# A threshold guess taken as a logarithm, its guards moved to VectorE, and a packed list's flags made by one comparison

## The chip, the cores and the metric

The kernel runs on one core of one Trainium2 chip. The metric is the device time of one execution in microseconds, lower is better. Engines are named as in the profile: PE (TensorE, with PEld for its weight loads), DVE (VectorE), ACT (ScalarE), POOL (GpSimd) and SP (SyncE, which here only issues transfers).

## The reference

A graph layer over 3327 nodes with 256 features each, run twice (two steps). In each step every node attends to all nodes, but only to its nucleus: the most probable nodes whose probabilities first reach 0.9 together. A sparse adjacency matrix diffuses the features beside it.

```python
h = jnp.maximum(_layernorm(x), 0.0)
Xf = Xa = h;  R = adj + eye;  R = R / R.sum(-1, keepdims=True)
for n in range(2):
    q = Xa @ W1.T @ W2.T;  k = Xa @ W3.T
    probs = softmax(q @ k.T)
    sp = sorted(probs, descending);  cs = cumsum(sp)
    keep = cs - sp < 0.9                       # the nucleus of each row
    A = probs * keep;  A = A / max(A.sum(-1, keepdims=True), 1e-12)
    Xf = R @ Xf
    Xa = A @ Xa
    Z = Z + Xf @ U1[n].T + Xa @ U2[n].T
return x + layernorm(h + Z) * ln_g + ln_b
```

All arithmetic is float32.

## The kernel before

**Tiles.** The nodes stand in 26 tiles of 128 rows, padded to 3328. A tile's attention row block is a 128 x 3328 array `e` of exponentials, made by matmuls (L600) and exponentials on ScalarE (L604 to L610).

**The nucleus without a sort.** For each tile the kernel guesses a threshold per row. `guessed` (L616) works out a first estimate from the row's sum of exponentials Z and from moments of the scores. Then ScalarE scans the whole row block against that estimate (`through`, L631, seen in the profile as L633): with Relu and with Sign, each with a sum. In the first step (`measured_once`, L635) these two sums give the guess col(16) by a short chain of one-column instructions; in the second step (`measured_twice`, L668) a third scan is made. The columns col(k) are the columns of one small tile `g` for each tile.

VectorE then clears everything at or over the guess and sums the rest (L729, in `settle`), takes the eight largest of each of 20 segments (L734), merges them (L738 to L753), and so finds the exact threshold; L763 clears `e` under it. If a guess was unfit for any row, a flag starts a slow layer that searches (`search_graph_layer`); the executions shown here do not enter it.

**The sum.** `Sums` transposes the cleared row block in seven parts on TensorE (L809), ScalarE copies each out (`eT`, L811), and TensorE multiplies it with the features (L823).

**The adjacency.** `listed` (L836) reads the adjacency matrix of each tile and lists per row the columns' blocks in which it has entries, up to 16; four are used directly. What is over these four is packed into one further list of 128 for the tile: L865 counts a row's entries, `packed` (L870) sums the counts over the rows before by a matmul and makes a 128 x 128 array of flags `oh` (which row a place of the packed list belongs to) by two comparisons on VectorE (L879, L880), `gathered` (L882) turns this into an index by a matmul. Indirect transfers that POOL issues then fetch the rows: `adjacent` (L896, seen as L900) and `fetched` (L917, seen as L921), five each for a tile. `diffuse` (L926) multiplies them.

**The order of the work** is written out by hand. In each iteration i of the loop at L1160 there are seven slots; a string for each slot (`PLAN` L1136, with others for the first and last iterations, L1141) names generators, and each letter runs one of them to its next `yield`:

- m: `measured` for tile i+1; d and c: `settle` for tile i and for the one before
- w and q: `weights` for tile i+3; e: `first_end` (L937), which ends tile i-2 (its copy `sv` L945 on ScalarE, the addition L946 on POOL)
- s: `spread`, the diffusion; a: `listed`; p: `packed` for tile i+1; h: `gathered` for tile i; g: one indirect transfer; o: a tile's own rows

After the letters of a slot a part of `Sums` is turned and one is summed. Each engine executes its instructions in the order in which this text issues them (L1232 makes that order binding for TensorE, ScalarE, VectorE and POOL, and in the first step for SP's queue). An indirect transfer issued by g also waits for the last ScalarE instruction that the text issued before it (L1206 to L1209).

For a tile of the first step `measured_once` has five segments. In the slots of `PLAN[0]`, counted from 0, they stand so: the estimate and its POOL columns in slot 0, the Relu scan in slot 1, the Sign scan in slot 3, the ScalarE chain L653 to L659 in slot 4, the five VectorE instructions L662 to L666 in slot 6. `settle` starts with L729 in slot 0 of the next iteration, and its L763 stands in slot 5.

Of the kernel before, what the change touches and what calls it, by code (L numbers as in the profile page):

```python
# [9 lines left out]
F32 = mybir.dt.float32  # L10
# [3 lines left out]
AF = mybir.ActivationFunctionType  # L14
ALU = mybir.AluOpType
# [3 lines left out]
P = 128  # L19
# [4 lines left out]
NP = NT * P  # L24
# [6 lines left out]

SCALE = 1.9
BITS = 27
FIRST = 2.0 ** -7
assert 0.1 * SCALE / N > 2.0 ** -15


# [1 line left out]
def search_graph_layer(  # L39
# [13 lines left out]
    nc = tc.nc  # L53
# [94 lines left out]
    def nucleus(es, z):  # L148
# [10 lines left out]
        nc.vector.memset(cand, FIRST)  # L159
# [153 lines left out]
BIG = 1.0e30  # L313
# [3 lines left out]
ROUNDS = (5, 6)  # L317
PG = (0.72168716, 3.51308980, -3.48705157)
PK = (3.57528079, -2.54929187, 0.86603878)
OFFSET = (18.0, 14.0)  # L320
TOPK = 8 * max(ROUNDS)
LNY = 0.25 * math.log(0.72)

# [6 lines left out]
FIRST = 8 * P  # L330
# [15 lines left out]
def guess_graph_layer(ctx, tc, x, adj, w1t, w2t, w3t, u1t, u2t, ln_g, ln_b, out, flag):  # L346
# [66 lines left out]
    one = const.tile([P, 8], F32, tag="one", name="one")  # L413
    for k, c in enumerate((1.0, -1.0, 5.0e-4, SQG[1], SQK[1], math.log(10.0), LNY, 1.0e-12)):
# [213 lines left out]
    def con(k):  # L628
        return one[:, k : k + 1]
# [5 lines left out]
    def measured_once(r):  # L635
        e, ms = r["e"], r["ms"]


        col = guessed(r, small.tile([P, 17], F32, tag="g", name="g"))
        S.activation(col(4), col(2), AF.Square, bias=con(4))  # L640
        S.activation(col(11), col(4), AF.Identity, scale=ms(5), bias=ms(6))
        S.activation(col(1), col(0), AF.Exp, scale=-1.0, bias=con(5))
        G.tensor_scalar(col(7), col(9), 0.5, None, ALU.mult)
        G.tensor_scalar(col(8), col(9), 0.5 * NP, None, ALU.mult)
        G.tensor_scalar(col(5), col(1), OFFSET[0], None, ALU.mult)
        G.tensor_scalar(col(10), col(9), col(5), 1.0, ALU.mult, ALU.add)
# [189 lines left out]
    def listed():  # L836
        pieces = [(t, j0, min(size, NT - j0)) for t in range(NT) for size in (HALF if t < HALVES else AD,)
                  for j0 in range(0, NT, size)]

        def asked(t, j0, n):  # L840
            at = (roomy[(2 * t + j0 // HALF) % 4] if t < HALVES else
                  adjp.tile([P, AD, P], F32, tag="at", name="at", bufs=2))
            nc.sync.dma_start(at[:, :n], adj[t, :, j0 : j0 + n, :])
            return at

        ahead = asked(*pieces[0])
        for k, (t, j0, n) in enumerate(pieces):
# [12 lines left out]
            V.max(ls[:, :8], fm)  # L860
            V.match_replace(fm, ls[:, :8], fm, 0.0)
            V.max(ls[:, 8:LIST], fm)
            G.tensor_scalar(index[:, t, :DIRECT], ls[:, :DIRECT], -1.0, float(NONE), ALU.mult, ALU.add)
            of = small.tile([P, LIST], F32, tag="of", name="of", bufs=2)
            V.tensor_scalar(of[:, DIRECT:], ls[:, DIRECT:LIST], 0.0, None, ALU.is_gt, ALU.add,  # L865
                            accum_out=over[:, t : t + 1])
            done.append(t)
            yield

    def packed(t):  # L870

# [4 lines left out]
        S.copy(ls[:, LIST:], pb[:, 0, :1])  # L876
        yield
        ohs[t] = oh = small.tile([P, P], F32, tag="oh", name="oh", bufs=2)
        V.tensor_scalar(oh, place, ov, ls[:, LIST:], ALU.subtract, ALU.is_lt)  # L879
        V.scalar_tensor_tensor(oh, place, ls[:, LIST:], oh, ALU.is_ge, ALU.mult)  # L880

    def gathered(t):  # L882
        oh = ohs.pop(t)
# [7 lines left out]
        yield  # L891
        of = small.tile([P, LIST], F32, tag="of", name="of", bufs=2)
        V.scalar_tensor_tensor(of[:, :n], place[:, :n], nth, lo, ALU.is_equal, ALU.mult, accum_out=nth)
        G.tensor_scalar(index[:, t, DIRECT:], nth, -1.0, float(NONE), ALU.mult, ALU.add)

    def adjacent(t):  # L896
# [83 lines left out]
        V.tensor_copy(flag, pf[:1, 0, :1])  # L980

    own_of = {}
    live, ohs, acs, xgs, done, early = {}, {}, {}, {}, [], {}
    none = iter(())

    def run(work, n=99):
# [139 lines left out]
    def refetch(t):  # L1126
# [14 lines left out]
    BEGIN = {-1: ("mba", "mmbba", "mwwbbaa", "bmwwb", "", "", ""),  # L1141
             0: ("mdbba", "mcdbba", "medbwwbap", "mdabb", "gmpdbwwba", "hgdabgbq", "hgq"),
             1: ("ggmdsssbba", "gmcdgsssbba", "gedbawwbp", "msdbga", "gmpdeag", "hgdawwqg", "hgemgqo"),
             2: ("gmdsssa", "gmcdsssga", "gedawwpg", "gmsdga", "gmspdea", "ohgdawwqg", "gehmgq")}
# [136 lines left out]
```

## Time and profile before

| what | value |
|---|---|
| median of 3 runs | 1354.68 us (1349.92 to 1356.13) |
| profiled execution, its own time | 1350.64 us |
| its span | 1348.9 us |
| busy: PE, DVE, ACT, POOL | 1268.1, 1186.8, 1081.0, 997.2 us |
| granted TensorE clock, mean | 0.982 |

The span is the time from the first to the last instruction of the profiled execution. Busy time is an engine's own; an engine may be busy and still wait for nothing, or idle and hold up nobody. The row of a group or of an instruction names line, engine, operation, what is written from what, and times. In the timeline the first number is the start in microseconds from the start of the span, the second the length; an idle time in front of an instruction is added in brackets with what ended it.

The first step fills the span from about 75 to 735 us; before it the features are normed and multiplied, from about 800 us the second step runs.

### The profile page before, as it was taken

The page shows a single profiled execution, that of the slowest core. Times are in us where ns is not written, and L with a number is a line of the kernel's source. Part 1 is how long each engine was busy: PE and PEld are TensorE (multiplying, and loading weights), DVE is VectorE, ACT ScalarE, POOL GpSimd, SP SyncE. Part 2 cuts the span into 40 slices and gives each one's busy share as a digit, 9 for nine tenths or more (in the row PEclk, how much of TensorE's full clock was granted, in tenths as well). Part 3 has the DMA queues.
Part 4 walks back from the last instruction along what each step waited for, and adds up shares of the span by engine and source line. Part 5 has one row for each costly group of instructions (what it writes and reads, how often), then busy time and mean ns, then how long its engine had stood idle before and what let it go on. Part 6 is the DMA issues. An engine that isn't in the chain of part 4 may idle for free.

```text
span 1348.9 us, 22270 instructions
## 1 busy us (share of the span) xinstructions
PE 1268.1 (94%) x6495; PEld 976.0 (72%) x6495; DVE 1186.8 (88%) x3637; ACT 1081.0 (80%) x2368; POOL 997.2 (74%) x1399
## 2 busy tenths in 40 slices
PE   5989899999999999999999579999999999999985
PEld 4635687877778777787877457777777777777774
DVE  6877899999999999999990689899998999999993
ACT  5475788798888879888863789899998999999841
POOL 5114788888878878887873578888888888888832
PEclk9999999999999999999999779999999999999998
DMA  8644545455454544445332212221212222122200
GB/s 277 221 157 141 160 136 144 134 144 147 133 153 133 140 138 142 144 135 152 106 104 86 75 55 60 78 89 54 91 59 85 62 82 90 52 91 64 81 21 24
DMA packets 92645, 149.79 MB, mean 111 GB/s; under 512 B 15425, under 2 KB 59072, under 8 KB 92512
## 3 DMA queue, kind: packets, MB, share of 16 engines
q1 hardware_dynamic: 75056, 105.37, 24.6%
q0 software_dynamic: 16640, 42.69, 12.1%
q8 instruction: 54, 0.88, 0.3%
q14 instruction: 79, 0.65, 0.2%
q10 hardware_dynamic: 816, 0.20, 0.1%
HBM read 120.93 MB, written 27.28 MB: 110 GB/s over the span
## 4 chain that ended last, share of the span: by engine, by line
PE 51%; DVE 20%; ACT 12%; POOL 11%; issue 3%; DMA 2%; SPq 0%; POOLq 0%; DVEq 0%; ACTq 0%
PE pa L823 22%; ACT ja L633 7%; PE pl L600 7%; PE pt L809 6%; PE pr L929 5%; POOL xg L921 5%; DVE w L729 4%; PE pz L942 3%; DVE cand L734 3%; DVE e L763 3%; PE pz L1011 2%; POOL g L676 2%; DVE bb L741 1%; DVE cand L743 1%; ACT e L604 1%
## 5 line engine op out<-in xcount | busy, mean ns | idle before, releaser
L823 PE MATMUL pa<-xw,eT 128*128 128x256 f32 x1352 | 323.6, 384 | 3.6 <-DVE s L953 3.6
L633 ACT ACTIVATE ja<-e,g 128x3328 uint8<-128x3328 f32 x106 | 325.7, 3072 | 0.1
L823 PE MATMUL pa<-x,eT 128*128 128x256 f32 x1352 | 323.1, 380 | 0.0
L823 PEld LDWEIGHTS pa<-xw,eT 128*128 128x128 f32 x1352 | 250.7, 190 | 52.5 <-issue 14.4
L823 PEld LDWEIGHTS pa<-x,eT 128*128 128x128 f32 x1352 | 243.7, 191 | 25.8
L734 DVE MAX8 cand<-w 128x8 f32<-128x168 f32 (+1 forms) x1040 | 253.7, 319 | 0.0
L811 ACT COPY eT<-pt 128x512 f32<-128x512 f32 (+1 forms) x364 | 199.5, 555 | 48.8 <-PE pt L809 47.7
L921 POOL DMA_INDIRECT xg<-bx,index x130 | 188.7, 1451 | 54.7 <-issue 24.4
L900 POOL DMA_INDIRECT ac<-in_adj,index x130 | 162.9, 1253 | 63.8 <-issue 28.2
L809 PE MATMUL pt<-ident,e 128*128 128x128 f32 x1144 | 176.6, 277 | 17.3 <-DVE e L760 9.4
L809 PEld LDWEIGHTS pt<-ident,e 128*128 128x128 f32 x1144 | 139.8, 144 | 60.5 <-issue 36.0
L921 POOL DMA_INDIRECT xg<-vx,index x130 | 152.5, 1173 | 34.3 <-issue 30.3
L729 DVE SCALAR_TENSOR_TENSOR w<-e,g 128x3328 f32<-128x3328 f32 x44 | 162.7, 3698 | 3.1 <-ACT g L714 3.0
L929 PE MATMUL pr<-xg,ac 128*128 128x257 f32 (+1 forms) x520 | 141.0, 395 | 8.4 <-DVE s L1119 6.8
L763 DVE SCALAR_TENSOR_TENSOR e<-e,rec 128x3328 f32<-128x3328 f32 x40 | 148.3, 3707 | 0.6
L604 ACT ACTIVATE e<-pl 128x832 f32<-128x832 f32 x132 | 112.9, 859 | 27.3 <-PE pl L600 21.9
L929 PEld LDWEIGHTS pr<-xg,ac 128*128 128x128 f32 x520 | 93.9, 194 | 34.0 <-issue 14.1
L600 PE MATMUL pl<-both,qT 64*128 64x416 f32 x416 | 93.0, 546 | 9.3 <-ACT e L604 7.0
L741 DVE MAX8 bb<-cand 128x8 f32<-128x160 f32 x286 | 92.7, 324 | 6.4
L853 DVE TENSOR_REDUCE fm<-at 128x4 f32<-128x512 f32 (+1 forms) x133 | 84.7, 637 | 13.3 <-DMA at<-in_adj 13.3
L600 PE MATMUL pl<-after,qT 64*128 64x416 f32 x416 | 95.4, 552 | 0.5 <-ACT e L604 0.5
L633 ACT ACTIVATE ja<-x,g 128x3328 uint8<-128x3328 f32 x24 | 73.7, 3070 | 0.0
(260 smaller groups left out, 2129.8 us busy)
## 6 DMA issues: line engine op xcount, KB each, us to landing
at<-in_adj SPq DMA_DIRECT2D x114, 256.0 KB
cx<-ac SPq DMA_DIRECT2D x26, 384.0 KB
ac<-cx SPq DMA_DIRECT2D x26, 384.0 KB
wide<-in_adj SPq DMA_DIRECT2D x8, 832.0 KB
e<-in_adj SPq DMA_DIRECT2D x6, 832.0 KB
own<-bx SPq DMA_DIRECT2D x26, 128.5 KB
x<-in_x SPq DMA_DIRECT2D x13, 256.0 KB
xr<-in_x SPq DMA_DIRECT2D x26, 128.0 KB
```

The source lines that it names most:

```text
L600: PE.matmul(pl[:, a, :wd], qT[p, :], keys_of(step, a).rearrange("p a b -> p (a b)")[:, c : c + wd], start=True, stop=True)
L604: S.activation(e.rearrange("p (a n) -> p a n", a=2)[:, :, c : c + wd], pl[:, :, :wd], AF.Exp, accum_out=za[:, n : n + 1])
L633: S.activation(ja, e, f, bias=guess, scale=sign, accum_out=total)
L729: V.scalar_tensor_tensor(w, e, col(16), e, ALU.is_lt, ALU.mult, accum_out=d2)
L734: V.max(cand[:, 8 * s : 8 * s + 8], w[:, s * SEG : min(NP, (s + 1) * SEG)])
L763: V.scalar_tensor_tensor(e, e, at(1), e, ALU.is_ge, ALU.mult, accum_out=ra)
L809: PE.transpose(pt[:, j, :], e[:, (j0 + j) * P : (j0 + j + 1) * P], ident)
L811: S.copy(eT[:, :w, :], pt[:, :w, :])
L823: PE.matmul(self.pa, eT[:, c - 4 * k, :], self.xa[:, j, :], start=c == 0, stop=c == NT - 1)
L900: G.indirect_dma_start(out=ac[:, k, :], out_offset=None, in_=rows, in_offset=bass.IndirectOffsetOnAxis(ap=index[:, t, k : k + 1], axis=0), ...
L921: G.indirect_dma_start(out=xg[:, k, :w], out_offset=None, in_=rows, in_offset=bass.IndirectOffsetOnAxis(ap=index[:, t, k : k + 1], axis=0))
L929: PE.matmul(pr[:, :w], ac[:, k, :], own if k == KT - 1 else xg[:, k, :w], start=k == 0, stop=k == KT - 1)
```

## The change

In the first step the guess is formed as a logarithm. Before, ScalarE took a power by Ln and Exp of a difference, and VectorE then limited it, multiplied it with the estimate and added guards (a huge number where the row is not to be cut). Now the logarithm of col(10) is taken by ScalarE behind the Relu scan (L654), the guards are made by three VectorE instructions (L663 to L665) as amounts to be subtracted from an exponent of at most 80, and ScalarE forms Relu and Exp from them (L666, L667). Four columns are added on POOL (L643, L648 to L650). The last segment moves from slot 6 to slot 5 and so stands ahead of `settle`'s clearing pass (L763 before, L764 after).

For the packed list the count of L865 on VectorE becomes a Sign with a sum on ScalarE (`counted`, L874), followed by two POOL instructions that make two limits of it (L876, L877). `gathered` for tile t runs it for tile t+2, in slot 6. In `packed` ScalarE adds one more instruction (L887) and a square over 128 x 128 places (L889), and VectorE makes the flags by one comparison (L891) in place of two.

One constant changes (18 to 19), and a name in the layer that is not entered. The line numbers of the changed kernel are higher by up to 13 from there on.

```diff
@@ measured_once
         S.activation(col(1), col(0), AF.Exp, scale=-1.0, bias=con(5))
+        G.tensor_scalar(col(11), col(11), -1.0, None, ALU.mult)
         G.tensor_scalar(col(7), col(9), 0.5, None, ALU.mult)
         G.tensor_scalar(col(8), col(9), 0.5 * NP, None, ALU.mult)
         G.tensor_scalar(col(5), col(1), OFFSET[0], None, ALU.mult)
         G.tensor_scalar(col(10), col(9), col(5), 1.0, ALU.mult, ALU.add)
+        G.tensor_scalar(col(12), col(3), ms(3), ms(8), ALU.mult, ALU.add)
+        G.tensor_scalar(col(12), col(12), -1.0, 80.0, ALU.mult, ALU.add)
+        G.tensor_scalar(col(13), r["Z"], 0.035, None, ALU.mult)
         yield
         oa = small.tile([P, 3], F32, tag="oa", name="oa")
         through(e, AF.Relu, col(9), -1.0, oa[:, 0:1])
+        S.activation(col(10), col(10), AF.Ln)
         yield
         through(e, AF.Sign, col(9), -1.0, oa[:, 1:2])
         yield
         S.activation(col(3), oa[:, 0:1], AF.Identity, scale=-1.0, bias=col(8))
         S.activation(col(4), oa[:, 1:2], AF.Relu, scale=col(7), bias=col(3))
         S.activation(col(6), col(4), AF.Ln, scale=col(1), bias=con(2))
-        S.activation(col(3), col(4), AF.Square, scale=col(1), bias=con(1))
-        S.activation(col(3), col(3), AF.Ln, scale=0.5, bias=col(10))
-        S.activation(col(3), col(3), AF.Identity, scale=-1.0, bias=col(6))
-        S.activation(col(3), col(3), AF.Exp, scale=col(11))
-        yield
-
-        V.tensor_scalar(col(5), oa[:, 1:2], NP - 31.0, BIG, ALU.is_gt, ALU.mult)
-        V.tensor_scalar(col(6), col(4), col(1), 0.35, ALU.mult, ALU.is_lt)
-        V.scalar_tensor_tensor(col(5), col(6), BIG, col(5), ALU.mult, ALU.add)
-        V.tensor_scalar(col(3), col(3), 1.0e20, col(9), ALU.min, ALU.mult)
-        V.tensor_tensor(col(16), col(3), col(5), ALU.add)
+        S.activation(col(10), col(10), AF.Identity, scale=-1.0, bias=col(6))
+        yield
+        V.tensor_scalar(col(5), oa[:, 1:2], NP - 31.0, 60.0, ALU.is_gt, ALU.mult)
+        V.tensor_scalar(col(14), col(4), col(13), 60.0, ALU.is_lt, ALU.mult)
+        V.scalar_tensor_tensor(col(12), col(12), col(5), col(14), ALU.subtract, ALU.subtract)
+        S.activation(col(10), col(10), AF.Relu, scale=col(11), bias=col(12))
+        S.activation(col(16), col(10), AF.Exp, scale=-1.0, bias=con(8))
@@ listed
-            of = small.tile([P, LIST], F32, tag="of", name="of", bufs=2)
-            V.tensor_scalar(of[:, DIRECT:], ls[:, DIRECT:LIST], 0.0, None, ALU.is_gt, ALU.add,
-                            accum_out=over[:, t : t + 1])
@@ new, and packed
+    def counted(t):
+
+        if t not in done or t in nhs:
+            return
+        of = small.tile([P, LIST], F32, tag="of", name="of", bufs=2)
+        ov = over[:, t : t + 1]
+        S.activation(of[:, DIRECT:], lists[:, t, DIRECT:LIST], AF.Sign, accum_out=ov)
+        nhs[t] = nh = small.tile([P, 3], F32, tag="nh", name="nh", bufs=4)
+        G.tensor_scalar(nh[:, 0:1], ov, -0.5, 0.5, ALU.mult, ALU.add)
+        G.tensor_scalar(nh[:, 1:2], ov, ov, 0.25, ALU.mult, ALU.mult)
     def packed(t):
-        assert t in done
+        counted(t)
+        nh = nhs[t]
...
         S.copy(ls[:, LIST:], pb[:, 0, :1])
-        yield
+        S.activation(nh[:, 2:3], pb[:, 0, :1], AF.Identity, scale=-1.0, bias=nh[:, 0:1])
         ohs[t] = oh = small.tile([P, P], F32, tag="oh", name="oh", bufs=2)
-        V.tensor_scalar(oh, place, ov, ls[:, LIST:], ALU.subtract, ALU.is_lt)
-        V.scalar_tensor_tensor(oh, place, ls[:, LIST:], oh, ALU.is_ge, ALU.mult)
+        S.activation(oh, place, AF.Square, bias=nh[:, 2:3])
+        yield
+        V.tensor_scalar(oh, oh, nh[:, 1:2], None, ALU.is_lt)
@@ gathered, behind its V.scalar_tensor_tensor
+        if valid(t + 2):
+            counted(t + 2)
@@ the order of the first step (the same in BEGIN 0 to 2)
-    PLAN = (("gmdsssa", "gmcdsssa", "edawwpg", "gmsdga", "gmspdea", "ohgdawwqg", "gehmgq"),
+    PLAN = (("gmdsssa", "gmcdsssa", "edawwpg", "gmsdga", "gmspdea", "ohgmdawwqg", "gehmgq"),
```

More of the change, by code (lines that the diff above doesn't have):

```diff
@@ L33 @@
 BITS = 27
-FIRST = 2.0 ** -7
+LOWEST = 2.0 ** -7
 assert 0.1 * SCALE / N > 2.0 ** -15
@@ L158, in nucleus @@
         nc.vector.tensor_scalar(thr, z, TOP_P, None, ALU.mult)
-        nc.vector.memset(cand, FIRST)
+        nc.vector.memset(cand, LOWEST)
         for k in range(BITS - 1, -1, -1):
@@ L319 @@
 PK = (3.57528079, -2.54929187, 0.86603878)
-OFFSET = (18.0, 14.0)
+OFFSET = (19.0, 14.0)
 TOPK = 8 * max(ROUNDS)
@@ L412, in guess_graph_layer @@
     law = const.tile([P, 7, NT], F32, tag="law", name="law")
-    one = const.tile([P, 8], F32, tag="one", name="one")
-    for k, c in enumerate((1.0, -1.0, 5.0e-4, SQG[1], SQK[1], math.log(10.0), LNY, 1.0e-12)):
+    one = const.tile([P, 9], F32, tag="one", name="one")
+    for k, c in enumerate((1.0, -1.0, 5.0e-4, SQG[1], SQK[1], math.log(10.0), LNY, 1.0e-12, 80.0)):
         G.memset(one[:, k : k + 1], c)
@@ L876, in packed @@
         S.copy(ls[:, LIST:], pb[:, 0, :1])
+        S.activation(nh[:, 2:3], pb[:, 0, :1], AF.Identity, scale=-1.0, bias=nh[:, 0:1])
+        ohs[t] = oh = small.tile([P, P], F32, tag="oh", name="oh", bufs=2)
+        S.activation(oh, place, AF.Square, bias=nh[:, 2:3])
         yield
-        ohs[t] = oh = small.tile([P, P], F32, tag="oh", name="oh", bufs=2)
-        V.tensor_scalar(oh, place, ov, ls[:, LIST:], ALU.subtract, ALU.is_lt)
-        V.scalar_tensor_tensor(oh, place, ls[:, LIST:], oh, ALU.is_ge, ALU.mult)
+        V.tensor_scalar(oh, oh, nh[:, 1:2], None, ALU.is_lt)
     def gathered(t):
@@ L982, in guess_graph_layer @@
     own_of = {}
-    live, ohs, acs, xgs, done, early = {}, {}, {}, {}, [], {}
+    live, ohs, acs, xgs, done, nhs, early = {}, {}, {}, {}, [], {}, {}
     none = iter(())
@@ L1141, in guess_graph_layer @@
     BEGIN = {-1: ("mba", "mmbba", "mwwbbaa", "bmwwb", "", "", ""),
-             0: ("mdbba", "mcdbba", "medbwwbap", "mdabb", "gmpdbwwba", "hgdabgbq", "hgq"),
-             1: ("ggmdsssbba", "gmcdgsssbba", "gedbawwbp", "msdbga", "gmpdeag", "hgdawwqg", "hgemgqo"),
-             2: ("gmdsssa", "gmcdsssga", "gedawwpg", "gmsdga", "gmspdea", "ohgdawwqg", "gehmgq")}
+             0: ("mdbba", "mcdbba", "medbwwbap", "mdabb", "gmpdbwwba", "hgmdabgbq", "hgq"),
+             1: ("ggmdsssbba", "gmcdgsssbba", "gedbawwbp", "msdbga", "gmpdeag", "hgmdawwqg", "hgemgqo"),
+             2: ("gmdsssa", "gmcdsssga", "gedawwpg", "gmsdga", "gmspdea", "ohgmdawwqg", "gehmgq")}
     OPEN = {-1: ("llcmss", "lnms", "lwwnfd", "lcmdsssggggg", "fmgdswqdf", "llmdf", "lmwfdm"),
```

## The prediction

> **What bounds the kernel now.** I read the busy shares first, then the table of stretches, TensorE's waits by stretch, and then ScalarE and GpSimd side by side in the timeline of one tile.
>
> ```profile
> PE 1268.1 (94%) x6495; PEld 976.0 (72%) x6495; DVE 1186.8 (88%) x3637; ACT 1081.0 (80%) x2368; POOL 997.2 (74%) x1399
> ```
> ```profile
> 300.00:400.00 100.00, 100.00 (x533) 79.47 (x532) 96.27 (x308) 85.86 (x209) 82.59 (x101) 1.00 0.49 141
> 400.00:500.00 100.00, 100.00 (x536) 79.02 (x535) 95.99 (x289) 84.97 (x213) 81.16 (x96) 1.00 0.50 144
> ```
>
> The second fence gives, for two stretches of the first step, length, then busy time of PE, PEld, DVE, ACT and POOL. The change touches only the first step (about 75 to 735 us). From 152 us to the end of that step TensorE is busy throughout: its waits between 200 and 700 us are an empty list, and the chain of waits there is made of TensorE's matmuls alone. Over tiles 4 to 24 the first scan ends every 23.77 us on average (22.95 and 24.60 in turn, the same to 0.01 us: TensorE's clockwork). So an engine that gets lighter gains nothing here; the question is whether another engine becomes slower than 23.77 us a tile. The 82% of POOL hides that. Tile 9, ScalarE and then GpSimd (start, length, engine, line):
>
> ```profile
> 294.45 3.06 ACT L633 ACTIVATE ja<-e,g 128x3328 uint8<-128x3328 f32 x1
> 297.41 0.19 ACT L633 ACTIVATION_READ_ACCUMULATOR ja<-e,g 128x1 f32 x1
> 297.50 0.57 ACT L811 COPY eT<-pt 128x512 f32<-128x512 f32 x1
> 297.97 0.38 ACT L477 COPY xT<-pt 128x256 f32<-128x256 f32 x1
> ```
> ```profile
> 298.28 1.10 POOL L900 DMA_INDIRECT ac<-in_adj,index  x1 [0.17 <-ACT eT L811]
> 299.39 0.48 POOL L906 TENSOR_TENSOR ac<-ac,ident 128x128 f32<-128x128 f32 x1
> 299.82 0.27 POOL L643 TENSOR_SCALAR g<-g 128x1 f32<-128x1 f32 x1
> 300.16 0.21 POOL L644 TENSOR_SCALAR g<-g 128x1 f32<-128x1 f32 x1
> 300.45 0.21 POOL L645 TENSOR_SCALAR g<-g 128x1 f32<-128x1 f32 x1
> 300.76 0.26 POOL L646 TENSOR_SCALAR g<-g 128x1 f32<-128x1 f32 x1
> 301.43 1.02 POOL L921 DMA_INDIRECT xg<-bx,index  x1 [0.41 <-ACT eT L811]
> ```
>
> The reader is to see two things. POOL's instructions stand end to end, with only the 0.3 us or so that each issue costs between them. And L646, which makes col(10), ends at 301.02, 3.5 us after ScalarE's first scan of the same tile has ended (297.51). Before the change nobody needs col(10) until L657, which starts at 305.94. I compared these two ends for every tile from 4 to 25: L646 is later by 1.6 to 5.0 us each time.
>
> Why POOL is full shows in the two long VectorE passes of a tile, each with the POOL instruction that started into it:
>
> ```profile
> 307.24 3.68 DVE L763 SCALAR_TENSOR_TENSOR e<-e,rec 128x3328 f32<-128x3328 f32 x1
> ...
> 312.30 3.68 DVE L729 SCALAR_TENSOR_TENSOR w<-e,g 128x3328 f32<-128x3328 f32 x1
> ```
> ```profile
> 307.72 3.78 POOL L946 TENSOR_TENSOR sv<-sv,x 128x256 f32<-128x256 f32 x1
> ...
> 312.92 3.88 POOL L921 DMA_INDIRECT xg<-bx,index  x1 [0.30 <-issue]
> ```
>
> L946 takes 0.75 us where no such pass runs (452.75), L921 0.95 us; here both last until the pass is over. That costs POOL 4 to 6 us a tile. In the ten tiles in which no gap of POOL exceeds 0.42 us (5 to 12, 14, 16), so that it runs on its own work alone, its period is 23.6 us: 0.2 us below TensorE's.
>
> **What the Trainium skill says.** "SBUF — State Buffer", section "Who interferes with whom": VectorE and GpSimd share a port pair under an exclusive lock, also taken by a VectorE instruction with two SBUF inputs, and the later one blocks. The trace agrees: 3.78 us in place of 0.75. "Perfetto Trace Analysis", section "GPSIMD Engine Instruction": GpSimd spans are not to be trusted; take the spacing of starts. I do: L643 to L646 start 0.33, 0.29 and 0.31 us apart, so a small POOL instruction costs 0.31 us, not the 0.21 of its row. The same page, section "Tensor Engine Instruction (MATMUL, LD_WEIGHTS)", calls the queues of ScalarE, VectorE and GpSimd strict FIFO, which is what makes a wait on one of them matter; on every engine the rows of this trace stand in the order of the text.
>
> **The change part by part, a tile.**
>
> VectorE: five guard instructions (311.46 to 312.15, 0.69 us) become three (0.41); the count L865 goes (0.17 + 0.08); L879 and L880 (0.34 + 0.35) become one. Together 0.9 us less. Worth nothing from 152 us on: TensorE's 100% covers it.
>
> TensorE and the SP queue: the same instructions in the same order.
>
> ScalarE: the chain L653 to L659 (2.49 us) becomes four instructions (1.5 by the spacing of L653 to L656), so 1.0 less. Added: the early logarithm L654 (0.29, from L659), the limit L887 (0.27, from L890) and the 128x128 square (0.3, near the copy L528): 0.85. Further the Relu and Exp behind the guards (0.3 each) and the count by Sign (0.3). ScalarE is at 85%, so this fits; but the Relu waits for VectorE's guards. They stand in slot 5 ahead of L763, and L763 starts about when ScalarE finishes sv, while ScalarE has still eT, lo and nth to do (over 1 us) before that Relu. I cost this wait at nothing, and at 0.3 us if VectorE is late.
>
> POOL: six more instructions (L643, L648 to L650, and the limits L876 and L877), 6 x 0.31 = 1.9 us. The indirect DMAs are the same ten a tile in the same order, some of them held back by a different last ScalarE instruction; none of these comes later than POOL does. The limits run ahead of the index L907 and of the fifth xg gather, which are needed an iteration later: only their length counts.
>
> The new wait: L654 on ScalarE, straight after the first scan, takes the logarithm of col(10), POOL's fifth instruction of this group. On the numbers of tile 9 it would wait from 297.5 to at least 301.3 (one POOL instruction more ahead of it). Queued behind it on ScalarE are the eT copy, xT, both exponentials of slot 2 and the second scan; TensorE waits for that eT to get a PSUM buffer for pb, and for its matmuls. POOL in turn is held behind ScalarE's second scan and needs sv (L945, now L958) for L946. So there is now a closed loop: sv on ScalarE, POOL to col(10), ScalarE's L654, on to the next sv. Before, this loop was open at L654.
>
> Its length, from the eight tiles in which POOL started L946 within 0.1 us of the end of sv (13, 14, 16 to 19, 21, 22): scan's end to sv's end 9.72 us on average, sv's end to L646's end 16.33; sum 26.05. Add three POOL instructions that stand within it (0.93), take off 0.1 for ScalarE (1.0 less, 0.85 more). The guards now hold L763 until ScalarE's chain ends, while it started up to 1.8 us before sv's end; a later L763 locks POOL longer: 0 to 0.8 us, I take 0.3. Loop: 27.2 us. Against 23.77 that is 3.4 us a tile; from tile 3 to tile 25 there are 22 steps: 75 us.
>
> Start and end: before 152 us TensorE waited 4.0 us for VectorE (L763 2.9, a copy of products 1.1); the lighter VectorE may save some of it, a guard that ScalarE now waits for in tiles 0 and 1 (VectorE starts them at 77.8, ScalarE is ready at about 75) may cost 3 us. I take 0, and keep -4 to +4. The second step has no changed instruction.
>
> Sum: the profiled execution took 1350.64 us (span 1348.9), which makes 1426; it lies 4 us under the median of the runs shown, 1354.68, so I say **1430**.
>
> **The rivals.**
>
> (a) POOL alone is the bound, and ScalarE's wait is absorbed. Then a tile takes POOL's free period plus its new work, 23.6 + 1.9 = 25.5, 1.7 more than TensorE: 22 x 1.7 = 37 us, 1392. For it: locks can shrink when POOL waits anyway. Against: the loop holds both locks, and POOL waited little.
>
> (b) Not slower: POOL gets ahead. Its lock time of 4 to 6 us depends on where VectorE's two passes fall; a VectorE lighter by 0.9 us moves them. If POOL reached col(10) 3.3 us earlier in each tile (the mean lag of those eight tiles, 2.4, and 0.9 of new work), L654 would not wait, TensorE would keep its 23.77, and only the start would move: 1350 to 1355. From that point on the change costs nothing. Against it: the passes keep their number and length, POOL's new work eats 1.9 us of such a gain, and in 22 tiles of 22 the lag was above 1.5 us.
>
> (c) The loop is longer than I make it (TensorE, kept waiting, is late for ScalarE in turn): above 4.6 us a tile, over 1456. I see no such return path, since ScalarE finds both score buffers ready after its wait. A failed proof, which would start the search layer, is in here too; nothing in the trace prices it.
>
> **How the numbers follow.** Forecast 0.60 (3.4 us a tile, 2 to 4.6 with its bounds), (a) 0.25, (b) 0.11, (c) 0.04. Half a per cent, 7 us, is about what a measurement of this kernel can tell from no change. (b) gives 0.05 faster and 0.06 same; slower is 0.89. The range takes in the forecast's bounds and most of (a): 1382 to 1458.
>
> **What would show it.** Right: in the changed profile ScalarE's L654 stands after an idle time of 2 to 5 us released by POOL g L647, in nearly every tile; TensorE falls to about 87% between 200 and 700 us; the first scan recurs about every 27 us; the second step keeps its length. For (a): a period near 25.5, POOL without gaps, little idle time at L654. Wrong altogether: no idle time at L654, TensorE still at 100% and 23.77 us a tile; then the lag of POOL was a matter of where VectorE's passes fell.

## The result, and the profile after

The changed kernel takes **1431.05 us** (median of 4 runs, 1426.07 to 1439.81) against 1355.41 us before (4 runs, 1349.92 to 1357.63). The ratio is 1.058, 95% interval 1.055 to 1.062: it is slower by 75.6 us. In the profiled execution (1426.07 us) the span is 1424.3 us, 75.4 more than the 1348.9 of before. The sums of this section are made between these two spans.

First the busy shares, in the form in which the prediction shows those of before:

```profile
PE 1291.1 (91%) x6495; PEld 991.5 (70%) x6495; DVE 1167.5 (82%) x3507; ACT 1097.0 (77%) x2472; POOL 1024.2 (72%) x1556
```

VectorE did get lighter (1186.8 to 1167.5 us), ScalarE and POOL got more instructions, and no engine is as full as before. That is what a loop of waits looks like from far off: everybody has idle time. The table of stretches (length, then busy time of PE, PEld, DVE, ACT, POOL, then clock and DMA) shows it in the first step:

```profile
300.00:400.00 100.00, 93.32 (x480) 74.13 (x481) 82.44 (x238) 79.24 (x211) 77.71 (x104) 0.97 0.43 124
400.00:500.00 100.00, 89.18 (x445) 70.14 (x444) 80.45 (x246) 76.08 (x188) 73.12 (x112) 0.93 0.45 125
```

TensorE was at 100.00 in both and is now at 93 and 89, with about 50 and 90 matmuls fewer in each hundred microseconds. The chain of work that ended last, by engine, says the same of the whole span: TensorE's share, 51% before, falls to that of VectorE.

```profile
DVE 25%; PE 25%; ACT 18%; POOL 16%; issue 5%; DMA 0%; POOLq 0%; DVEq 0%; SPq 0%; ACTq 0%
```

Next, who waits for whom between 230 and 690 us (line, what it waited for, us in total, times, longest), TensorE's row first, then ScalarE's. This list held no row of TensorE before.

```profile
PE pb L885 <- ACT eT L812: 34.1, 17, 4.4
...
ACT g L654 <- POOL g L647: 47.3, 17, 5.4
```

And the rows that wait in L654 over the whole execution, from the answer for that one source line:

```profile
L654 ACT ACTIVATE g<-g x26: 185/203/204, 66.2 to 754.8; 128x1 f32<-128x1 f32 x26
its engine sat idle before it (us, times) until:
  POOL g L647: 71.4, 24
```

An instruction of 0.2 us for one column makes ScalarE stand still for 71.4 us, in 24 tiles of 26. Tile 8 in the timeline, ScalarE and then POOL (start, length, engine, line; in brackets the idle time ahead and what ended it):

```profile
294.70 3.06 ACT L633 ACTIVATE ja<-e,g 128x3328 uint8<-128x3328 f32 x1
297.67 0.20 ACT L633 ACTIVATION_READ_ACCUMULATOR ja<-e,g 128x1 f32 x1
300.27 0.20 ACT L654 ACTIVATE g<-g 128x1 f32<-128x1 f32 x1 [2.40 <-POOL g L647]
300.38 0.57 ACT L812 COPY eT<-pt 128x512 f32<-128x512 f32 x1
301.11 0.88 ACT L604 ACTIVATE e<-pl 128x832 f32<-128x832 f32 x1
...
303.94 3.07 ACT L633 ACTIVATE ja<-e,g 128x3328 uint8<-128x3328 f32 x1
306.91 0.19 ACT L633 ACTIVATION_READ_ACCUMULATOR ja<-e,g 128x1 f32 x1
...
309.09 0.37 ACT L958 COPY sv<-pz 128x256 f32<-128x256 f32 x1
...
326.36 0.20 ACT L654 ACTIVATE g<-g 128x1 f32<-128x1 f32 x1 [3.61 <-POOL g L647]
```
```profile
298.87 0.27 POOL L643 TENSOR_SCALAR g<-g 128x1 f32<-128x1 f32 x1
...
299.97 0.26 POOL L647 TENSOR_SCALAR g<-g 128x1 f32<-128x1 f32 x1
...
307.37 0.95 POOL L913 DMA_INDIRECT ac<-in_adj,index  x1 [1.26 <-ACT ja L633]
...
309.60 3.39 POOL L959 TENSOR_TENSOR sv<-sv,x 128x256 f32<-128x256 f32 x1
...
314.42 3.51 POOL L934 DMA_INDIRECT xg<-bx,index  x1 [0.30 <-issue]
...
326.06 0.26 POOL L647 TENSOR_SCALAR g<-g 128x1 f32<-128x1 f32 x1
```

The reader can walk round the loop here: the scan has ended at 297.87, the logarithm waits to 300.27 for col(10) (L647, ends at 300.23); eT, the exponentials, the second scan and sv follow it in ScalarE's order without a gap; POOL's gather L913, like every indirect transfer, waits for the last ScalarE instruction issued before it, which is that scan (its end is at 307.10), L959 starts at 309.60, just after sv, and with its two locked instructions POOL reaches the next tile's L647 only at 326.06. That one again ends a wait of L654, 3.61 us this time.

So each of the two engines waits for the other in every round. On POOL's side the wait stands at the gather behind the second scan, and hardly ever at L959 (POOL's waits, 230 to 690 us):

```profile
POOL ac L913 <- ACT ja L633: 22.2, 17, 1.3
POOL ac L913 <- ACT oh L889: 21.9, 17, 1.4
...
POOL sv L959 <- ACT sv L958: 2.4, 2, 1.2
```

For tiles 3 to 24, L959 starts within 0.14 us of the end of sv in 16 tiles of 22, so there both ways round are about equally long; in the other six it starts 3.3 to 3.8 us later, and of the two only the second scan holds POOL. The second row is a wait for the new square L889; POOL would have to stop for the scan afterwards in any case.

**Where the 75.4 us are.** Taking the end of the first scan (without the reading of its sum) as the mark of a tile: it comes at 163.09 us in place of 152.95 for tile 3 (10.1 later), then 590.1 us pass to tile 25 in place of 524.7 (65.4 more, 2.97 for each of 22 steps), and from there to the end it is 671.1 against 671.2 us. So 10.1 at the start, 65.4 in the loop, nothing in the rest.

### The profile page after: what moved, and what is told of

It is laid out like the page before. It is cut to its first block, busy times and chain, and to the rows that moved or that the text cites. A ratio compares the mean times of both kernels' runs of the same rounds, so it can differ in the third digit from the quotient of the medians.

```text
span 1424.3 us, 22425 instructions
## 1 busy us (share of the span) xinstructions
PE 1291.1 (91%) x6495; PEld 991.5 (70%) x6495; DVE 1167.5 (82%) x3507; ACT 1097.0 (77%) x2472; POOL 1024.2 (72%) x1556
## 4 chain that ended last, share of the span: by engine, by line
DVE 25%; PE 25%; ACT 18%; POOL 16%; issue 5%; DMA 0%; POOLq 0%; DVEq 0%; SPq 0%; ACTq 0%
PE pa L824 13%; ACT ja L633 8%; POOL xg L934 6%; DVE w L730 6%; DVE cand L735 4%; DVE e L764 4%; PE pt L810 3%; PE pz L955 3%; ACT eT L812 2%; PE pl L600 2%; POOL ac L913 2%; DVE x L764 2%; DVE bb L742 2%; ACT e L604 2%; DVE cand L744 2%
## 5 line engine op out<-in xcount | busy, mean ns | idle before, releaser
L824 PE MATMUL pa<-x,eT 128*128 128x256 f32 x1352 | 339.2, 395 | 0.0
L824 PEld LDWEIGHTS pa<-x,eT 128*128 128x128 f32 x1352 | 254.9, 200 | 29.8
L934 POOL DMA_INDIRECT xg<-bx,index x130 | 191.7, 1475 | 58.8 <-issue 17.7
L913 POOL DMA_INDIRECT ac<-in_adj,index x130 | 143.6, 1105 | 95.1 <-ACT oh L889 27.6
L810 PE MATMUL pt<-ident,e 128*128 128x128 f32 x1144 | 181.5, 282 | 24.4 <-DVE e L761 9.5
L934 POOL DMA_INDIRECT xg<-vx,index x130 | 133.7, 1029 | 34.0 <-issue 29.8
L764 DVE SCALAR_TENSOR_TENSOR e<-e,rec 128x3328 f32<-128x3328 f32 x40 | 147.4, 3686 | 0.6
L854 DVE TENSOR_REDUCE fm<-at 128x4 f32<-128x512 f32 (+1 forms) x133 | 84.4, 635 | 15.9 <-DMA at<-in_adj 15.9
L678 POOL TENSOR_SCALAR g<-g 128x1 f32<-128x1 f32 x26 | 73.4, 2822 | 1.8
```

Of the source, the lines that this page charges most:

```text
L764: V.scalar_tensor_tensor(e, e, at(1), e, ALU.is_ge, ALU.mult, accum_out=ra)
L810: PE.transpose(pt[:, j, :], e[:, (j0 + j) * P : (j0 + j + 1) * P], ident)
L824: PE.matmul(self.pa, eT[:, c - 4 * k, :], self.xa[:, j, :], start=c == 0, stop=c == NT - 1)
L913: G.indirect_dma_start(out=ac[:, k, :], out_offset=None, in_=rows, in_offset=bass.IndirectOffsetOnAxis(ap=index[:, t, k : k + 1], axis=0), ...
L934: G.indirect_dma_start(out=xg[:, k, :w], out_offset=None, in_=rows, in_offset=bass.IndirectOffsetOnAxis(ap=index[:, t, k : k + 1], axis=0))
```

## The experiments

Theory: the loop over ScalarE's early logarithm and POOL's order costs 3 us a tile and nearly everything. Rivals: POOL's added work alone; the guards that ScalarE waits for; TensorE's clock, which the records show at half speed after some of the new stalls. The ratios are to the kernel before, each against runs on its own chip; the period is that of the profiled execution, mean of tiles 3 to 25.

| kernel | median us | ratio (95%) | period us |
|---|---|---|---|
| before (first profile) | 1354.68 | 1 | 23.85 |
| the change | 1431.05 | 1.058 (1.055 to 1.062) | 26.82 |
| e1: before, early logarithm alone | 1398.91 | 1.033 (1.031 to 1.036) | 25.71 |
| e2: before, POOL's six instructions alone | 1373.17 | 1.014 (1.012 to 1.016) | 24.69 |
| e3: the change, logarithm in slot 4 | 1381.28 | 1.019 (1.017 to 1.020) | 25.04 |
| e4: the change, col(10) first on POOL | 1416.16 | 1.045 (1.043 to 1.047) | 26.27 |
| e5: guess part alone | 1412.16 | 1.044 (1.041 to 1.047) | 26.00 |
| e6: packed part alone | 1354.22 | 1.001 (0.9995 to 1.002) | 24.07 |
| e7: guess part, logarithm late, columns on VectorE | 1381.11 | 1.019 (1.017 to 1.022) | 24.50 |
| e8: the change, TensorE's stalls filled | 1433.49 | 1.059 (1.056 to 1.061) | 26.97 |
| e9: the change, Relu and Exp in slot 6 | 1445.60 | 1.068 (1.064 to 1.073) | 27.63 |
| e10: e7 with the columns ahead of the guards, Relu and Exp in slot 6 | 1368.58 | 1.011 (1.007 to 1.015) | 24.73 |
| e11: e10 with the packed part | 1367.76 | 1.010 (1.007 to 1.013) | 24.53 |
| e12: e11, Relu and Exp at the end of slot 5 | 1359.83 | 1.006 (1.004 to 1.007) | 24.23 |

**e1, the wait alone.** The kernel before gets one unused instruction, so that nothing changes but the wait.

```diff
         through(e, AF.Relu, col(9), -1.0, oa[:, 0:1])
+        S.activation(col(12), col(10), AF.Ln)
```

> The kernel before with one instruction more in a tile of the first step: a logarithm of col(10) on ScalarE behind the Relu scan, its result unused. Loop theory: it closes the loop between ScalarE and GpSimd. Loop = 26.05 us (measured before) + 0.3 for the logarithm = 26.3 us against 23.77, 22 steps of 2.5 us: +56 us, about 1411. Rival (GpSimd's six more instructions are the whole cost): nothing, GpSimd has no more work here, within 4 us of the kernel before, about 1355. Third (ScalarE has 15% idle time and swallows the wait): the same 1355, with the idle time seen in front of the logarithm but TensorE still at 100%.

Measured 1398.91, 44 us slower. The waits between 230 and 690 us, TensorE and ScalarE:

```profile
PE pb L876 <- ACT eT L812: 17.9, 10, 2.4
...
ACT g L650 <- POOL g L646: 31.7, 18, 3.4
```

The same two rows as in the change, with a 0.2 us instruction as the only edit. The wait alone makes more than half of the loss, though 12 us less than the 1411 that I expected of it. The expectation took the way over sv, with the addition L946 locked. Here POOL starts this addition 2.05 to 2.64 us after sv has ended, and it takes 0.74 us (tiles 3 to 24), so the loop doesn't run over sv at all. POOL's wait is the one behind the second scan:

```profile
POOL ac L901 <- ACT ja L633: 22.9, 19, 1.4
```

**e2, POOL's work alone.** The kernel before, with six unused instructions on POOL in the places of the six new ones.

```diff
+        G.tensor_scalar(col(12), col(11), -1.0, None, ALU.mult)
         G.tensor_scalar(col(7), col(9), 0.5, None, ALU.mult)
...
+        G.tensor_scalar(col(13), col(3), ms(3), ms(8), ALU.mult, ALU.add)
+        G.tensor_scalar(col(13), col(13), -1.0, 80.0, ALU.mult, ALU.add)
+        G.tensor_scalar(col(14), r["Z"], 0.035, None, ALU.mult)
...
+            G.tensor_scalar(nh[:, 0:1], ov, -0.5, 0.5, ALU.mult, ALU.add)
+            G.tensor_scalar(nh[:, 1:2], ov, ov, 0.25, ALU.mult, ALU.mult)
```

> The kernel before with the six GpSimd instructions of the change (four in the group that makes col(10), one of them ahead of it, and two behind the gathers, on the count that VectorE makes), their results unused; nobody waits for them. Loop theory: the loop stays open, GpSimd alone becomes the bound: its free period 23.6 + 6 x 0.31 = 25.5 us a tile against 23.77, 22 steps of 1.7 us: +37 us, about 1392. Rival (GpSimd's load is the whole cost): +76, 1431. Third (only the wait costs): 1355.

Measured 1373.17: slower by 18 us, half of what I expected. POOL now hardly waits (0.1 us a tile beyond its issue gaps) and is the bound, but how it slows the others is in ScalarE's waits (230 to 690 us):

```profile
ACT g L657 <- POOL g L648: 36.5, 19, 3.3
```

L657 is the Identity in slot 4. It reads col(8) and writes col(3), and one of the six, L648, still has to read the old col(3). Tile 10, POOL and then ScalarE:

```profile
331.67 0.21 POOL L645 TENSOR_SCALAR g<-g 128x1 f32<-128x1 f32 x1
...
332.67 0.34 POOL L648 TENSOR_SCALAR g<-g,ms 128x1 f32<-128x1 f32 x1
```
```profile
333.04 0.29 ACT L657 ACTIVATE g<-oa,g 128x1 f32<-128x1 f32 x1 [1.85 <-POOL g L648]
```

L645, which makes col(8), had ended 1.16 us before L657 started, L648 0.03 us before, and in every one of these waits it is the same (1.0 us or more, and 0.03). So "nobody waits for them" was wrong: the copied instruction brought a wait of its own, for a column to be free, and it binds because POOL has fallen 8.0 us behind the first scan (2.9 before). The dependence on col(8) was there all along; by itself it would have made each of these waits 1.0 us or more shorter. As POOL is full, I take its load to set the pace and this wait to be only the place where ScalarE feels it; a run with the write moved to another column would show it, and was not made.

**e3, the logarithm late.** The change with one instruction moved down, into the chain in which its result is used.

```diff
         through(e, AF.Relu, col(9), -1.0, oa[:, 0:1])
-        S.activation(col(10), col(10), AF.Ln)
...
         S.activation(col(6), col(4), AF.Ln, scale=col(1), bias=con(2))
+        S.activation(col(10), col(10), AF.Ln)
         S.activation(col(10), col(10), AF.Identity, scale=-1.0, bias=col(6))
```

> The changed kernel with its logarithm of col(10) moved from behind the Relu scan to the ScalarE chain of slot 4, just ahead of the Identity that uses it. Loop theory: ScalarE reaches it some 8 us after the scan's end, GpSimd is 3 us late, so the wait goes and GpSimd's load remains: 25.5 us a tile, about 1392; as VectorE is lighter its locks may fall otherwise, 1380 to 1400. Rival (GpSimd's load is the whole cost): 1431 as in the changed kernel. Third (only the wait costs): 1355 or less.

Measured 1381.28. The place of one instruction is worth 50 of the 76 us. What stays is e2's state, with the same wait for col(3) (ScalarE's waits, 230 to 690 us), POOL 8.5 us behind, and a start that is 5.6 us late:

```profile
ACT g L657 <- POOL g L648: 32.1, 18, 2.5
```

**e4, col(10) first.** The change, with L646 and L647 (col(5), col(10)) ahead of POOL's other columns, so three instructions earlier.

```diff
         S.activation(col(1), col(0), AF.Exp, scale=-1.0, bias=con(5))
+        G.tensor_scalar(col(5), col(1), OFFSET[0], None, ALU.mult)
+        G.tensor_scalar(col(10), col(9), col(5), 1.0, ALU.mult, ALU.add)
         G.tensor_scalar(col(11), col(11), -1.0, None, ALU.mult)
         G.tensor_scalar(col(7), col(9), 0.5, None, ALU.mult)
         G.tensor_scalar(col(8), col(9), 0.5 * NP, None, ALU.mult)
-        G.tensor_scalar(col(5), col(1), OFFSET[0], None, ALU.mult)
-        G.tensor_scalar(col(10), col(9), col(5), 1.0, ALU.mult, ALU.add)
```

> The changed kernel with the order of its GpSimd group altered: col(5) and col(10) first, then the other six. The work of every engine is the same. Loop theory: three instructions of 0.31 us leave the loop, 26.8 - 0.9 = 25.9 us a tile, 22 x 0.9 = 20 us less: about 1411; not under GpSimd's own 25.5. Rival (GpSimd's load is the whole cost): 1431, unchanged, since the load is.

Measured 1416.16: 15 us back by the medians (11 by the profiled spans), 0.55 us a tile from three small instructions taken out of the loop. L654 still waits for what is now L644 (36.8 us in 17 waits). Taking them out of the loop is worth 0.18 us each, not the 0.3 I had counted.

**e5 and e6, the two parts apart.** e5 has the guess as changed and the packed list as before; e6 the reverse. Here e5 against the change, cut to its core; e6 takes the other half of the diff.

```diff
-        S.activation(of[:, DIRECT:], lists[:, t, DIRECT:LIST], AF.Sign, accum_out=ov)
...
-        G.tensor_scalar(nh[:, 0:1], ov, -0.5, 0.5, ALU.mult, ALU.add)
-        G.tensor_scalar(nh[:, 1:2], ov, ov, 0.25, ALU.mult, ALU.mult)
...
-        V.tensor_scalar(oh, oh, nh[:, 1:2], None, ALU.is_lt)
+        V.tensor_scalar(oh, place, ov, ls[:, LIST:], ALU.subtract, ALU.is_lt)
+        V.scalar_tensor_tensor(oh, place, ls[:, LIST:], oh, ALU.is_ge, ALU.mult)
```

> The changed kernel with the packed list made as before (count and two comparisons on VectorE): only the guess as a logarithm is left of the change. Loop theory: the loop measured before (26.05 us) gains one GpSimd instruction and the logarithm (0.3 each) and loses 1.0 us of ScalarE's chain: 25.7 us; the run with the wait alone showed 25.7 where the same sum gave 26.3, so 25.0 to 25.7: 22 x 1.2 to 1.9 us, 1381 to 1397. Rival (the packed part's limits and its square on ScalarE are what costs): 1355 to 1360.

> The kernel before with only the packed list's part of the change (count on ScalarE, two limits on GpSimd, the square on ScalarE, one comparison on VectorE). Loop theory: no new wait of ScalarE on GpSimd that binds; two GpSimd instructions, which cost 0.2 us each in the run with six of them: GpSimd's period 23.6 + 0.4 = 24.0 against 23.77: +5 us, 1360. Rival (the packed part costs by its ScalarE work): 1380 or more.

Measured 1412.16 and 1354.22. e5 misses its expectation by 15 us and more, above all because the expectation left the start out, which is 9.8 us late here too. e6 is free within 0.2%, where I had expected some 5 us. TensorE's one row of waits in it, between 230 and 690 us:

```profile
PE pt L809 <- DVE e L763: 0.5, 1, 0.5
```

The packed part's two POOL instructions bring POOL 5.8 us behind the scan, and ScalarE waits for POOL only once in this stretch (1.3 us, for col(8)). The parts don't add (58 and 0 make 76): the loop of e5 takes 26.00 us, that of the whole change 26.82. I read this so, without a run of its own: in e6 the packed part's work falls into slack, in the change it stands inside the closed loop and lengthens it.

**e7, the guess with its costs taken out.** Logarithm in slot 4, the four new columns on VectorE behind the Relu scan, packed list as before.

```diff
-        G.tensor_scalar(col(11), col(11), -1.0, None, ALU.mult)
...
         through(e, AF.Relu, col(9), -1.0, oa[:, 0:1])
-        S.activation(col(10), col(10), AF.Ln)
+        V.tensor_scalar(col(11), col(11), -1.0, None, ALU.mult)
+        V.tensor_scalar(col(12), col(3), ms(3), ms(8), ALU.mult, ALU.add)
+        V.tensor_scalar(col(12), col(12), -1.0, 80.0, ALU.mult, ALU.add)
+        V.tensor_scalar(col(13), r["Z"], 0.035, None, ALU.mult)
```

> The guess part of the change without the two costs: the logarithm stands in slot 4, the four added GpSimd columns are made by VectorE behind the Relu scan, the packed list is made as before. GpSimd has exactly the work of the kernel before and ScalarE no new wait. Loop theory with TensorE as the bound: 23.77 us a tile again, 1350 to 1357, TensorE at 100% between 230 and 690 us. Rival (the place of the guards, ahead of the clearing pass, costs by itself): over 1360.

Measured 1381.11: a miss. With the loop and POOL's work both gone, 27 us are still lost, 13.5 of them ahead of tile 3. ScalarE's waits from 72 to 165 us:

```profile
ACT g L666 <- DVE g L665: 12.9, 3, 8.8
```

Relu (L666) waits for VectorE's guards, and the exponentials behind it with it: the third one of tile 1 starts at 83.0 us (76.7 before). So the wait for the guards is a third cost. In the change it shows at the start alone (6.9 us in three waits). How much of it belongs to the change is not settled by e7: the longest wait ends when VectorE makes the guards at 82.0 us (75.2 in the change), because VectorE had stood before them in waits for adjacency rows, and in the steady loop e7's own first column on VectorE waits for ScalarE, 8.0 us in ten waits between 230 and 690 us.

**e8, TensorE's stalls filled.** The trace's clock records show TensorE at half clock for 41.0 us between 157 and 760 us, in ten spells that stand beside the new stalls; in the kernel before there were none between 152 us and the end of its first step. In e8 TensorE makes the score matmuls of slot 2 twice, to have work at hand.

```diff
-            for a in range(2):
+            for a in (0, 1) * (2 if step == 0 and n < 2 and t > 3 else 1):
```

> The changed kernel, in which TensorE makes the scores of slot 2 twice (the same matmuls into the same place, 1.6 us more work in a tile from tile 4 on), just ahead of pb, where it stalls. It asks how much of the loss is the TensorE clock, which the changed kernel's trace shows at half for 41 us of the first step, always near a stall of 1.8 us or more. Clock theory: stalls get shorter by up to 1.6 us, the half clock goes from most tiles, 10 to 20 us less: 1411 to 1421, in spite of more work. Rival (the clock only falls in time that is lost anyway): 1431 or some us more.

Measured 1433.49, no gain. TensorE's wait at the pb matmul halves (34.1 to 15.9 us, 230 to 690 us), the half clock falls to 27.3 us, and ScalarE's wait for POOL is as long as ever (47.3 before the filling, 50.4 with it). So TensorE's slow clock falls into time that the loop has lost already. Some half clock was left, and the doubled matmuls are work of their own, so this speaks for what was taken away, a third of it.

**e9, the two behind the guards in a slot of their own.** The change with a yield ahead of Relu and Exp, which puts them into slot 6.

```diff
+        yield
         S.activation(col(10), col(10), AF.Relu, scale=col(11), bias=col(12))
         S.activation(col(16), col(10), AF.Exp, scale=-1.0, bias=con(8))
```

> The changed kernel with the Relu and Exp behind the guards in a segment of their own, one slot later, so that ScalarE no longer waits for VectorE's guards in the middle of slot 5. Third-cost theory: the changed kernel loses 10 us before the first scan of tile 3 ends (163.1 against 153.0 us), because at tile 0 the third exponential stands behind that wait (3.5 us); 6 to 10 us come back: 1421 to 1425. The loop at the early logarithm is untouched: no more than that. Rival (the start is lost at the logarithm of tile 2, which waits 6.2 us): 1431, nothing comes back.

Measured 1445.60, slower still. The start doesn't move (tile 3 at 162.70 against 163.09), though Relu's wait there falls from 6.9 to 0.7 us, so in the change the late start was not ScalarE's wait for the guards alone. And col(16), now made later, holds up VectorE's mask (230 to 690 us):

```profile
DVE w L731 <- ACT g L668: 35.1, 12, 3.1
```

**e10 and e11, all three costs taken out.** Logarithm late; the four columns on VectorE directly ahead of the guards; Relu and Exp in slot 6. ScalarE's chain writes col(15) in place of col(3), so that it overwrites nothing that the new columns still read. e10 keeps the packed list as before, e11 has the whole change. Against e7, without the lines of col(15):

```diff
         through(e, AF.Relu, col(9), -1.0, oa[:, 0:1])
-        V.tensor_scalar(col(11), col(11), -1.0, None, ALU.mult)
...
         yield
+        V.tensor_scalar(col(11), col(11), -1.0, None, ALU.mult)
...
         V.scalar_tensor_tensor(col(12), col(12), col(5), col(14), ALU.subtract, ALU.subtract)
+        yield
         S.activation(col(10), col(10), AF.Relu, scale=col(11), bias=col(12))
```

> The guess part with all three costs taken out: the logarithm in slot 4, the four added columns on VectorE directly ahead of the guards (where nothing has to be waited for), Relu and Exp in a segment of their own; the packed list as before. Third-cost theory: the 0.5 us a tile that TensorE waited for mq in the run with the guess on VectorE and the 13 us at its start go: 1350 to 1358. Rival (the guards ahead of the clearing pass cost by themselves): 1375 or more.

> The whole change (guess and packed list) with the three costs taken out as in the guess alone. TensorE as the bound: 23.8 us a tile, the packed part was free by itself: 1350 to 1358, no better than the kernel before by more than 0.3%, since TensorE has the same work. Rival (with the two limits GpSimd falls behind again): 1362 to 1372.

Measured 1368.58 and 1367.76: less lost than in any form of the guess part so far, but not nothing. The start is nearly right (tile 3 at 156.1 and 155.2). In e11 the mask still waits, 12.7 us in 13 waits for L668.

**e12, the same at the end of slot 5.** Relu and Exp stand behind the exponentials, qT and mq of slot 5, and not in slot 6. The string of slot 5 in PLAN against e11; those of iterations 1 and 2 get the same letter.

```diff
-"ohgmdawwqg"
+"ohgmdawwqgm"
```

> The whole change with its costs taken out as in the run before (logarithm in the chain of slot 4, the four limit columns on VectorE), but Relu and Exp behind the guards stand at the end of slot 5, after the exponentials, qT and mq, in place of slot 6. In the run before VectorE's mask waited for ScalarE's Exp in slot 6 for 12.7 us in thirteen waits between 230 and 690 us; at the end of slot 5 that wait should go and mq should not be late either. Theory: these waits were most of what was still lost: 1352 to 1360 us, TensorE near 100% between 230 and 690 us. Rival: what is left comes from the four columns more on VectorE and from the guards in front of the clearing pass, wherever the two ScalarE instructions stand: 1364 to 1372 us.

Measured 1359.83, at the edge of what the theory gave. The mask's wait is down to 1.0 us, and TensorE is nearly full again (stretches, columns as above):

```profile
300.00:400.00 100.00, 98.53 (x524) 77.92 (x523) 93.84 (x294) 86.27 (x223) 84.98 (x107) 1.00 0.47 138
400.00:500.00 100.00, 99.22 (x524) 77.80 (x523) 96.18 (x300) 86.91 (x223) 84.69 (x110) 1.00 0.48 141
```

Two ScalarE instructions a few places earlier are worth 6 to 8 us (by the ratios and by the medians). About 5 us of 460 are left as TensorE's waits (2.4 for the clearing pass, 1.6 for mq, 1.0 in two others); the remaining 0.55% (0.38 to 0.72%) against the kernel before was not resolved further. No version beats the kernel before.

## Why the prediction was right

**The bound.** TensorE's 100% did cover the lighter VectorE: in e6, where VectorE has 12 us less to do (1174.5 against 1186.8), TensorE's clockwork kept the time.

**The mechanism.** L654 waits for L647 in nearly every tile, 2.9 us on average over the 22 steps (2 to 5 was forecast), TensorE is at 89 to 95% in the stretches between 200 and 700 us (87), the period is 26.8 (27.2), the second step keeps its length. e1 and e3 show the cause from both sides: put in alone, the wait costs 44 us; moved away, it gives back 50. The prediction named both ways in which POOL is held, the second scan and sv, and wrote the loop down over sv. POOL's waits between 230 and 690 us show the scan in all 17 rounds, and in e1, of these two, the scan alone. It was wrong in saying that no gate of an indirect transfer comes later than POOL does: the square L889 is one, though nothing shows that it lengthens the loop.

**The size: two errors that cancelled, which is luck.** The loop was put at 3.4 us a tile and is 2.97: 65 us in place of 75. By its parts: from the logarithm to sv's end 9.50 us (9.62 forecast), from there to L647's end 17.23 (17.56 forecast with its three POOL instructions and 0.3 of lock). The term that was mis-sized is POOL's: at the 0.2 us each that e2 and e4 show, three instructions are 0.6 us in place of 0.93, as much as the path is shorter; that the shortening is theirs is an estimate. The lock term was about right. In the eight tiles that the forecast starts from, sv's addition L946 took 3.03 us on average; L959 takes 3.21 in the 16 tiles in which it follows sv at once, and 0.74 in the other six. The Trainium skill, "SBUF — State Buffer", "Who interferes with whom", has VectorE and GpSimd share a port pair under an exclusive lock, which a VectorE instruction with two SBUF inputs also needs; the 3.39 us of L959 above, against 0.75 unlocked, agree.

The start was the other error, and its step failed: I took 0 with 4 us to both sides, and it is 10.1. I had looked there for VectorE's guards alone and not for the new wait, though tile 2 passes the same instruction. Its row for ScalarE, 72 to 165 us:

```profile
ACT g L654 <- POOL g L647: 6.2, 1, 6.2
```

With the logarithm late (e3) the start is 5.6 us late in place of 10.1; without the wait for the guards (e9) it stays. With both moved, and the columns on VectorE, it is 2.3 us late in e11 and not at all in e12 (152.59 against 152.95). This fits two waits that each delay the start where the other is gone, and so don't add; but in e1, with the early logarithm alone, the start loses only 1.3 us, and what makes the rest of e9's delay is not settled.

**Costed at nothing.** ScalarE's wait for the guards really costs nothing in the steady loop of the change: its list between 230 and 690 us has no row for L666. The cover I named was work of ScalarE behind sv; e7 shows that the cover was in part the loop itself: once it is open, there is a row for L666 (5.6 us in six waits), in a kernel that is 1.9% slower than before.

**POOL's price.** Six instructions at 0.31 us were too dear. In e2 POOL's period without its waits goes from 23.44 (23.85 less 0.41) to 24.58 us (24.69 less 0.11): 1.1 us for six, 0.2 each. The Trainium skill, "Perfetto Trace Analysis", "GPSIMD Engine Instruction", advises the spacing of starts, and the spacing here is 0.29 (the eight from L643 on in tile 8); what POOL lost in net time is less. Why is not shown.

**Rival (a)** did not happen in the change, where POOL waits 2.0 us a tile beyond its issue gaps. It is what remains when the loop is opened (e2, e3): POOL with 0.1 us of such waits a tile, at a period of 24.7 and 25.0 us where (a) said 25.5. Even there ScalarE's wait is not absorbed: POOL pulls ScalarE back in slot 4, over col(3), which ScalarE overwrites and L648 still reads. I had named one new dependence between the two engines where the change brings two, in slot 1 and in slot 4; the second shows no wait as long as the first is there. Of **rival (c)**, TensorE does wait for eT and its clock is halved beside these stalls, but no return path shows: ScalarE waits no longer for TensorE than before (38.7 us between 230 and 690 us, 52.5 before), and e8 gains nothing by filling the stalls. **Rival (b)** did not happen in any version that keeps the early logarithm. (Its mean lag of the eight tiles is 2.1 us, not 2.4; nothing rests on that.)

## What to carry to other kernels

Before an instruction is moved up in an in-order queue, compare the end of its producer with its new place in every tile, and in the first tiles apart. Look also at what a moved or added instruction still reads: whoever overwrites that column next must wait for it, even if nobody uses the result. A lag of 2 to 5 us on another engine, harmless so far, becomes a loop when the two engines already wait for each other somewhere else. A low busy share doesn't clear an engine: ask how far it runs behind the one that will wait for it, and which of its results is the next to bind. When several costs hide behind one another, taking out the largest shows the next, so sum the parts only after they have been run together.

## What the runs showed of the hardware

Short stalls can halve TensorE's clock. In the change the spells last 3.413 or 6.827 us and stand beside stalls of 1.8 to 4.4 us; in e1 one follows a stall of 1.73 us and another stall of 1.73 us has none, and in the change six stalls of 1.8 to 2.6 us have none. Length alone doesn't decide it, and what does is not shown. The Trainium skill, "TensorE: Matmul & The Clock Gate", "🔬 Part 1: The HAM clock gate (the "warmup" mystery)", gives half clock and a window of about 3.4 us, and both agree; it also has the clock fall after at least one idle window of that length, and here single stalls half as long were enough in some places.
